# The last batch of a six-stage decoder kernel: the first half's feed forward placed beside the second attention's last part, and more side steps beside the part before it

## The chip, the cores and the metric

The kernel runs on one core of a Trainium2 chip. The metric is the device time of one execution in microseconds (us), as the median of several runs. One execution was also taken by the hardware profiler; its instructions, waits and transfers are what the views quoted below show. Engines are named as the profile names them: PE (TensorE, matmul), PEld (its weight loads), DVE (VectorE), ACT (ScalarE), POOL (GpSimd), SP (SyncE, here a queue of transfers).

## The reference

Input x has 4 batches of 1024 tokens with 256 channels. Two layers follow, each with a self attention, a cross attention to 77 context tokens and a feed forward, all with a layer norm before them and a residual add after. What the change touches is the second layer:

```python
x = x + _L1_attn_ref(_layernorm(x), L1_attn_W)            # 16 heads, |q.k|^2 times a decay, causal
x = x + _L1_xattn_ref(_layernorm(x), ctx_768, ...)        # 8 heads, softmax over 77 context tokens
x = x + _L1_ffn_ref(_layernorm(x), w_gate, w_up, w_down)  # 256 -> 704 -> 256

def fp4_linear(x, w):                                     # blocks of 16, both sides rounded to FP4
    return jnp.einsum('bsk,nk->bsn', fp4_quant_dequant(x), fp4_quant_dequant(w))
...
h = jax.nn.silu(fp4_linear(x, w_gate)) * fp4_linear(x, w_up)
return fp4_linear(h, w_down)
```

The attention mixes tokens causally; the cross attention and the feed forward work on each token by itself. So the second half of a batch's tokens needs the first half in the attention, and nowhere after it.

## The kernel before

A tile is 128 tokens by 256 channels; a batch has eight, held in two halves of four (`X[b, 0]` and `X[b, 1]`). The stages are Python generators that emit instructions and yield after each *step*. `schedule` (end of the file) combines them: `weave(a, na, b, nb)` advances a and b so that after any number of steps their shares done/na and done/nb are level, `zip2` advances all its generators once per round, `chain` runs one after another, `take(g, n)` gives the next n steps of g. The text order that comes out is the planner's priority order: `TileContext(..., schedule_with_timeline_sim=True)` orders each engine's queue at build time, by a timeline of its own, among instructions whose inputs and buffers are ready there. On the chip each queue runs in that order.

The stages of the second layer:

- `A1` is the self attention, written as units of one key tile by a chunk of two query tiles. Chunk c has 2c+2 units; four head groups make a pass. For the last batch, b = 3, the passes are split: chunks 0 and 1 of all four groups first (24 units, the *short part*, first half of the tokens), then chunks 2 and 3 (56 units, the *long part*, second half). Per unit there are score matmuls (L898, banks S), absolute values (DVE L904, ACT L902), a square (ACT L906), on the diagonal a decay (POOL L909), and value matmuls (L927). Line L947 (POOL) adds a finished chunk of a group into X; there are eight in each part.
- `XA(b, 1, (half,))` is the cross attention of one half: layer norm, a transposed pair of high and low parts, then per tile a *head* (scores, eight exponentials on ACT, a division) and a *tail* (transposes, 15 matmuls, the residual add on DVE, L637). It is 9 steps.
- `F1(b, groups, alt, keep)` is the feed forward. Per group of nt tiles: layer norm on POOL (L206 to L212, L226), rounding to FP4 (`fp4`: L1005 to L1009 and L1011 to L1014, DVE, POOL and ACT in turns), transposes (L235). Per tile: *up*, 24 matmuls of 352 columns with a tanh, a copy and two products (L1094, L1095, L1097, L1099), FP4 rounding of the 704 values, and *down*: six transposes (L1109, L1113), their high and low parts (L179, L180), 18 matmuls of 256 columns, and the residual add on DVE, L1118. The group's store to `out` (L171) is issued after its last tile. A whole batch is 52 steps, a group of four alone 27, a group of two alone 15.
- `XF(K, b)` is what follows A1 for a batch: `XA` of half 0 (9 steps), then `XA` of half 1 zipped with the first 20 steps of `F1` (21 rounds), then the other 32 steps of `F1`: 62 steps.

`alt` renames the buffers that a stage uses, so that two can be under way at once. Lane banks are T and W (PSUM banks 4, 5, 6) by default, TB and WB (banks 0 to 3, which A1 uses for S, U and D) where `alt` has `ps` 1. `XL` gives the cross attention buffers of its own; `FL` has four sets for the feed forward: `FL[0]` is None (its own buffers xn, xX, E, xph, xpl, wst, kh, q4s), `FL[1]` puts the same into `ot`, `QS`, `V`, `y0`, `y1`, `P`, `KS`, `VsJ` with banks T and W, `FL[2]` and `FL[3]` use `DL`, `QS` or `KS`, `V`, `WAh`, `WAl`, `qp`, `P`, `VsJ` with banks TB and WB. QS, KS, P, VsJ, DL, y0, y1 and ot are A1's.

The last batch before the change, in text order:

1. Beside the short part: three units, then 21 units woven with 20 steps of `XF(2)`.
2. Beside the long part: three units, then the other units of A1 (weight 55) woven with the other 42 steps of `XF(2)`, zipped with `XA(3, 1, (0,))`: 43 rounds with weight 62, so they end in the text at about unit 38 of 55.
3. After A1: `XA(3, 1, (1,))` on banks TB and WB, then lanes 2 and 3 (feed forward of tiles 4, 5 and of tiles 6, 7) zipped; woven one to one with lanes 0 and 1 (tiles 0, 1 and tiles 2, 3) zipped.

Of the kernel before, what the change touches and what calls it, by code (L numbers as in the profile page):

```python
# [1136 lines left out]
def zip2(*gens):  # L1137
    gens = list(gens)
    while gens:
        for g in list(gens):  # L1140
            try:
                next(g)
            except StopIteration:
                gens.remove(g)
        yield


def run_all(g):
    for _ in g:
        pass  # L1150


def chain(*gens):
    for g in gens:
        yield from g


def take(g, n):
    for _ in range(n):
        if next(g, g) is g:  # L1160
            return
        yield


def weave(a, na, b, nb):

    live = {0: (a, na), 1: (b, nb)}
    done = [0, 0]
    while live:
        k = min(live, key=lambda k: done[k] / live[k][1])  # L1170
        try:
            next(live[k][0])
            done[k] += 1
        except StopIteration:
            del live[k]
        yield


def spill(K, b):
    K.n += 1  # L1180
    K.xs[b] = K.dr.tile([T, C], F32, name=f"xs{b}")
    for g in range(2):
        K.store_x(b, K.xs[b], g)
    yield


def XF(K, b):

    yield from K.XA(b, 1, (0,), K.XL)
    f1 = K.F1(b, keep=K.w1)  # L1190
    yield from zip2(late(lambda: K.XA(b, 1, (1,), K.XL, K.mu)), take(f1, 20))
    yield from f1
# [6 lines left out]
def schedule(K, nb):  # L1199
    K.prep_a0()  # L1200
    preps = chain(K.prep_x(0), K.prep_p0(), K.prep_x(1), K.prep_f0())
    front = K.A0_front(0, K.kept)
    run_all(take(front, NF0))
    K.prep_ctx()
    run_all(weave(front, 44 - NF0, take(preps, NP0), NP0))
    more = {1: K.prep_x(2), 2: chain(K.prep_a1(), K.prep_f1_up()), 3: K.prep_f1_down()}
    a1 = K.A1([(b, (0, 1, 2, 3)) for b in range(nb - 1)] + [(nb - 1, (0, 1)), (nb - 1, (2, 3))])
    for b in range(nb):
        seg = K.A0(b, K.A0_front(b + 1) if b + 1 < nb else chain(K.A1_front(0), take(a1, 1)))
        if b == 0:  # L1210
            side, n = preps, NS0
        else:
            side, n = chain(K.XA(b - 1, 0), K.F0(b - 1), spill(K, b - 1), more[b]), NS1[b - 1]
        run_all(weave(seg, 196, side, n))
    K.phase = 1
    for b in range(nb):
        side = chain(K.XA(nb - 1, 0), K.F0(nb - 1), spill(K, nb - 1)) if b == 0 else XF(K, b - 1)
        if b + 1 < nb:
            main = chain(take(a1, 44), weave(take(a1, 22), 22, K.A1_front(b + 1), 19), take(a1, 14))
            run_all(take(main, K.LAG1 + 1))  # L1220
            run_all(weave(main, 96, side, 85 if b == 0 else 68))
        else:
            run_all(take(a1, K.LAG1 + 1))
            xf = XF(K, b - 1)
            run_all(weave(take(a1, 21), 21, take(xf, 20), 20))
            run_all(take(a1, K.LAG1 + 1))
            run_all(weave(a1, 55, zip2(xf, K.XA(b, 1, (0,), K.XL)), 62))
    b = nb - 1

    def lanes(ks):  # L1230
        return zip2(*(K.F1(b, ((2 * k, 2),), K.FL[k], K.w1) for k in ks))

    run_all(weave(chain(K.XA(b, 1, (1,), {**K.XL, "ps": 1}), lanes((2, 3))), 1, lanes((0, 1)), 1))


def parts(K, phases, nb):
# [41 lines left out]
@with_exitstack  # L1278
def decoder_kernel(ctx, tc, ins, consts, out, phases=None, nb=B):
    K = Kern(ctx, tc, ins, out, consts, nb=nb)  # L1280
    if phases is None or len(phases) == 6:
        schedule(K, nb)
    else:
        parts(K, phases, nb)
# [41 lines left out]
```

## Time and profile before

| what | value |
|---|---|
| time, median of 3 runs | 2407.63 us |
| lowest and highest run | 2401.26, 2417.06 us |
| the profiled execution's own time | 2403.86 us |
| its span, first to last instruction | 2402.1 us |
| mean granted PE clock over the span | 0.955 |
| busy share of PE, DVE, ACT, POOL | 90%, 70%, 68%, 50% |
| last L947 (chunk of A1 added) of the short part | 2112.02 us |
| last L947 of the long part, the end of A1 | 2267.33 us |

The span runs from the first to the last instruction; the own time is 1.8 us more, the median of the runs 3.8 us more than the own time. In a row of the timeline the first number is the start in us from the span's start, the second the duration, then engine, line, operation, tiles written and read, shapes; brackets hold the idle time before it and what ended that. In the table by windows each row is a stretch, with the busy time of each engine in it and, at the end, the mean granted PE clock, the share of the DMA engines and GB/s.

### The profile page before, as it was taken

What the parts mean: (1) busy time and instruction counts of PE and PEld (TensorE: products, weight loads), DVE (VectorE), ACT (ScalarE), POOL (GpSimd) and SP (SyncE); (2) the same over time, 40 slices, a digit from 0 to 9 for tenths busy, and PEclk for the clock granted to TensorE, in tenths of its full rate; (3) what the DMA queues carried; (4) which work ended last, traced back from release to release, by engine and by line L of the source; (5) the groups of instructions that cost most, each with busy time, mean ns of one, the idle gap of its engine ahead of it and who ended that gap; (6) DMA issues with size and microseconds to landing.
All of it is one profiled execution on the core that took longest, in us unless ns stands there. A gap on an engine that the chain in (4) does not pass through costs nothing.

```text
span 2402.1 us, 51405 instructions
## 1 busy us (share of the span) xinstructions
PE 2150.0 (90%) x19073; PEld 1520.1 (63%) x19110; DVE 1688.9 (70%) x3781; ACT 1638.8 (68%) x4173; POOL 1196.0 (50%) x1942
## 2 busy tenths in 40 slices
PE   6798999998999998899988988889988998899886
PEld 5454457755667655576656766567766767676676
DVE  4666657677666787776765667777866777777775
ACT  4365446676766676565778878987678877887542
POOL 7121303154331352412545458766866787775664
PEclk9899999999999999899989999999999999899997
DMA  8677331224751236222262224412341223542000
GB/s 256 190 206 212 117 90 44 63 57 115 230 143 49 62 105 194 73 73 49 73 188 50 71 71 138 140 38 56 99 116 38 56 80 115 104 99 71 10 10 18
DMA packets 182697, 238.45 MB, mean 99 GB/s; under 512 B 16198, under 2 KB 165846, under 8 KB 175958
## 3 DMA queue, kind: packets, MB, share of 16 engines
q1 hardware_dynamic: 182446, 235.15, 34.9%
q8 instruction: 151, 2.47, 0.4%
q14 instruction: 100, 0.82, 0.1%
HBM read 152.62 MB, written 82.21 MB: 98 GB/s over the span
## 4 chain that ended last, share of the span: by engine, by line
PE 60%; DVE 13%; DMA 8%; ACT 7%; POOL 7%; issue 3%; SPq 1%; POOLq 0%; another core or an unknown queue 0%; ACTq 0%; DVEq 0%
PE T L191 10%; PE W L191 8%; PE O L413 7%; PE Q L191 5%; PE O L927 5%; PE S L401 4%; PE M L352 4%; PE S L898 3%; DVE P L904 2%; DVE s_mt L357 2%; PE W L630 1%; DMA wst<-in_L_xattn_Wq 1%; DMA KS<-c_alk 1%; ACT P L906 1%; PE T L723 1%
## 5 line engine op out<-in xcount | busy, mean ns | idle before, releaser
L357 DVE TENSOR_REDUCE s_mt<-M 128x1 f32<-128x512 f32 (+3 forms) x608 | 386.2, 656 | 135.1 <-PE M L356 97.3
L404 ACT ACTIVATE P<-S 128x512 f32<-128x512 f32 (+1 forms) x640 | 342.0, 562 | 152.3 <-PE S L401 77.0
L906 ACT ACTIVATE P<-P,eps 128x1024 f32<-128x1024 f32 x320 | 343.9, 1080 | 55.5 <-DVE P L904 52.6
L904 DVE TENSOR_REDUCE P<-S 128x512 f32<-128x512 f32 (+1 forms) x480 | 284.8, 611 | 78.2 <-PE S L898 58.6
L352 PE MATMUL M<-KS,QS 108*128 108x512 bf16 (+3 forms) x768 | 225.7, 339 | 47.8 <-DVE s_mt L357 24.6
L898 PE MATMUL S<-QS,KS 96*128 96x256 bf16 (+1 forms) x1280 | 219.4, 270 | 36.6 <-DVE P L904 34.1
L191 PE MATMUL T<-R,xX 128*128 128x352 f32 (+1 forms) x1136 | 246.5, 331 | 4.0 <-ACT E L619 1.4
L401 PE MATMUL S<-QS,KS 110*128 110x256 bf16 (+1 forms) x1280 | 230.4, 267 | 14.7 <-ACT P L404 12.4
L413 PE MATMUL O<-P,V 128*32 128x256 f32 (+1 forms) x2560 | 239.4, 376 | 0.5 <-ACT ot L427 0.2
L622 POOL TENSOR_TENSOR E<-E,s_xsm 128x616 f32<-128x616 f32 x64 | 77.8, 1217 | 323.9 <-DVE s_xsm L620 270.8
L191 PEld LDWEIGHTS T<-R,xX 128*128 128x128 f32 x1136 | 182.9, 190 | 24.1 <-ACT E L619 5.4
L191 PE MATMUL W<-R,xph 128*128 128x256 f32 (+1 forms) x952 | 184.8, 292 | 6.5 <-DVE xpl L180 4.8
L909 POOL TENSOR_TENSOR P<-P,y 128x512 f32<-128x512 f32 x128 | 164.8, 1296 | 31.8 <-ACT y L871 17.0
L619 ACT ACTIVATE E<-T,s_xmx 128x77 f32<-128x77 f32 x512 | 159.3, 333 | 28.1 <-DVE s_xmx L616 26.0
L927 PE MATMUL O<-P,VsJ 128*32 128x128 f32 x3584 | 170.4, 286 | 4.8 <-ACT P L906 3.8
L898 PEld LDWEIGHTS <-KS 96*128 96x128 bf16 x1280 | 102.1, 99 | 110.6 <-issue 88.9
L401 PEld LDWEIGHTS <-KS 110*128 110x128 bf16 x1280 | 106.9, 99 | 102.5 <-issue 58.6
L191 PEld LDWEIGHTS W<-R,xph 128*128 128x128 f32 (+1 forms) x952 | 149.1, 192 | 17.7 <-DVE xpl L180 6.6
L352 PEld LDWEIGHTS <-QS 108*128 108x128 bf16 x768 | 68.1, 99 | 126.5 <-issue 99.2
L191 PE MATMUL W<-R,xpl 128*128 128x256 f32 (+2 forms) x476 | 139.5, 293 | 0.8 <-DVE xpl L180 0.8
L730 POOL TENSOR_TENSOR R<-wst 128x256 f32<-128x256 f32 x128 | 92.9, 736 | 86.0 <-DVE wst L729 80.9
L179 ACT ACTIVATE xph<-W 128x512 fp32r<-128x512 f32 (+2 forms) x180 | 79.1, 457 | 83.1 <-PE W L633 34.0
(351 smaller groups left out, 5662.6 us busy)
## 6 DMA issues: line engine op xcount, KB each, us to landing
QS<-dr SPq DMA_DIRECT2D x144, 192.0 KB
KS<-dr SPq DMA_DIRECT2D x72, 384.0 KB
dr<-qp SPq DMA_DIRECT2D x32, 768.0 KB
MD<-R SPq DMA_DIRECT2D x24, 616.0 KB
UD<-R SPq DMA_DIRECT2D x24, 512.0 KB
R<-MD SPq DMA_DIRECT2D x32, 308.0 KB
X<-in_x SPq DMA_DIRECT2D x16, 512.0 KB
dr<-qp SPq DMA_DIRECT2D x32, 256.0 KB
```

Source lines behind the costliest of these rows:

```text
L191: nc.tensor.matmul(out, x, y, start=first and n == 0, stop=last and n == len(seq) - 1)
L352: nc.tensor.matmul(Sv[:, x, 0:w], QS[:108, i // 4, hh, i % 4 * 128 : i % 4 * 128 + 128], KS[:108, hh, k0:k1], start=x == 0, stop=not diag ...
L357: nc.vector.tensor_reduce(out, Sv[:, :, 0:w], AX.X, ALU.max)
L401: nc.tensor.matmul(S[:, e, 0:w], st[1][:110, hh, j * 128 : (j + 1) * 128], st[0][:110, q0 // 512, hh, q0 % 512 : q0 % 512 + w], start=e == ...
L404: nc.scalar.activation(P[:, 2 * p : 2 * p + 2, 256 - w :], S[:, :, 0:w], AF.Exp)
L413: nc.tensor.matmul(O[0][hh * 32 : hh * 32 + 32, o + o0 : o + 256], V[j // 4][:, j % 4, h * 17 : h * 17 + 32], P[:, hh, o0:], start=c % 2 = ...
L619: nc.scalar.activation(E[:, n * 77 : (n + 1) * 77], Sv[:, k, :], AF.Exp, bias=mx[:, n : n + 1], accum_out=sm[:, n : n + 1])
L898: nc.tensor.matmul(S[:, e, 0:w], st[r][1][:96, hh, j * 128 : (j + 1) * 128], st[r][0][:96, q0 // 512, hh, q0 % 512 : q0 % 512 + w], start= ...
L904: nc.vector.tensor_reduce(Pv, S[:, :, 0:w].unsqueeze(3), AX.X, ALU.max, apply_absolute_value=True)
L906: nc.scalar.activation(Pw, Pw, AF.Square, bias=self.eps1)
L909: nc.gpsimd.tensor_tensor(Pd, Pd, Ds[r, c][:, j - 2 * c], ALU.mult)
L927: nc.tensor.matmul(Oc[rows, o0 : o0 + 128], lhs, P[:, hh, c0 : c0 + 128], start=j == 2 * c and i == 2 * c, stop=fin and i == 2 * c + 1)
```

## The change

Three edits, all in `schedule`, for the last batch alone:

```diff
             xf = XF(K, b - 1)
-            run_all(weave(take(a1, 21), 21, take(xf, 20), 20))
+            run_all(weave(take(a1, 21), 21, take(xf, 36), 36))
             run_all(take(a1, K.LAG1 + 1))
-            run_all(weave(a1, 55, zip2(xf, K.XA(b, 1, (0,), K.XL)), 62))
+            side = chain(zip2(xf, K.XA(b, 1, (0,), K.XL)), K.F1(b, ((0, 4),), keep=K.w1))
+            run_all(weave(a1, 55, side, 57))
     b = nb - 1
 
-    def lanes(ks):
-        return zip2(*(K.F1(b, ((2 * k, 2),), K.FL[k], K.w1) for k in ks))
-
-    run_all(weave(chain(K.XA(b, 1, (1,), {**K.XL, "ps": 1}), lanes((2, 3))), 1, lanes((0, 1)), 1))
+    f1 = [K.F1(b, ((2 * k, 2),), K.FL[k], K.w1) for k in (2, 3)]
+    run_all(chain(K.XA(b, 1, (1,), {**K.XL, "ps": 1}), zip2(*f1)))
```

Beside the short part 36 steps of `XF(2)` are woven in place of 20: all of both cross attention halves, the feed forward of batch 2's first half, and the start of that of its second. Beside the long part there are the other 26 steps zipped with `XA(3, 1, (0,))` (27 rounds), then the feed forward of batch 3's first half as one group of four tiles in the default buffers (27 steps): 54 rounds with weight 57, so they end in the text at about unit 52 of 55. After A1 there are only `XA(3, 1, (1,))` and then lanes 2 and 3. `FL[0]` and `FL[1]` are used no more. The arithmetic is the same. The first half has one layer norm over four tiles in place of two over two, and one store in place of two.

## Prediction

> **What bounds the kernel now.** First the page: which engine is full, and where it stops being full.
>
> ```profile
> span 2402.1 us, 51405 instructions
> PE 2150.0 (90%) x19073; PEld 1520.1 (63%) x19110; DVE 1688.9 (70%) x3781; ACT 1638.8 (68%) x4173; POOL 1196.0 (50%) x1942
> ...
> PE   6798999998999998899988988889988998899886
> ...
> PEclk9899999999999999899989999999999999899997
> ```
>
> PE is the bound (90% busy, nines and eights in the slices) until the last slices, which fall to 8 and 6. Only the last 350 us are touched. Second, the table by windows, cut at the ends of A1's parts (2112 and 2267.3):
>
> ```profile
> 2055.00:2074.00 19.00, 17.62 (x195) 14.34 (x195) 13.97 (x37) 16.98 (x42) 16.93 (x29) 1.00 0.42 90
> 2074.00:2093.00 19.00, 15.70 (x183) 9.60 (x181) 15.75 (x36) 16.66 (x38) 16.59 (x32) 0.73 0.65 138
> 2093.00:2112.00 19.00, 18.26 (x199) 14.38 (x199) 14.05 (x39) 17.55 (x49) 13.67 (x23) 1.00 0.55 111
> 2112.00:2196.00 84.00, 81.22 (x893) 65.37 (x891) 62.97 (x140) 69.72 (x178) 58.40 (x104) 0.98 0.37 88
> 2196.00:2267.30 71.30, 64.34 (x723) 47.27 (x722) 55.99 (x120) 50.73 (x76) 39.74 (x67) 0.98 0.08 28
> 2267.30:2278.00 10.70, 4.56 (x28) 3.83 (x26) 6.13 (x14) 2.36 (x5) 10.06 (x18) 0.81 0.00 1
> 2278.00:2340.00 62.00, 51.34 (x337) 48.85 (x338) 45.34 (x101) 28.89 (x108) 42.47 (x60) 0.89 0.03 10
> 2340.00:2369.00 29.00, 22.66 (x141) 20.96 (x140) 24.18 (x40) 13.41 (x28) 19.74 (x16) 0.94 0.03 10
> 2369.00:2402.10 33.10, 20.04 (x102) 18.27 (x102) 12.31 (x25) 5.11 (x11) 8.78 (x7) 0.66 0.07 24
> ```
>
> The first busy column is PE. In the long part it is 81.22 + 64.34 = 145.6 of 155.3 us (94%): whatever is put there lengthens it almost one for one. In the 134.8 us after A1, the *tail*, it is 98.6 us (73%): 36 us are empty. The short part has one soft place, 2074 to 2093, with PE at 15.7 of 19 us and the clock at 0.73.
>
> Third, the timeline, for who is late:
>
> ```profile
> 2148.33 0.42 DVE L1118 SCALAR_TENSOR_TENSOR X<-W,X 128x256 f32<-128x256 f32 x1 [1.57 <-PE W L191]
> ...
> 2259.01 0.41 DVE L1118 SCALAR_TENSOR_TENSOR X<-W,X 128x256 f32<-128x256 f32 x1
> ...
> 2267.33 0.46 POOL L947 TENSOR_TENSOR X<-X,yy 128x128 f32<-128x128 f32 x1 [3.25 <-DVE yy L945]
> ...
> 2293.68 0.42 DVE L1118 SCALAR_TENSOR_TENSOR X<-W,X 128x256 f32<-128x256 f32 x1 [0.80 <-PE W L191]
> ...
> 2332.57 0.42 DVE L637 TENSOR_TENSOR X<-X,WB 128x256 f32<-128x256 f32 x1 [0.75 <-PE WB L191]
> ...
> 2398.45 0.42 DVE L1118 SCALAR_TENSOR_TENSOR X<-WB,X 128x256 f32<-128x256 f32 x1 [4.30 <-PE WB L191]
> ```
>
> The feed forward of batch 2 adds its first tile at 2148.3, its fifth at 2259.0, and its eighth at 2293.7, 26 us after A1 (2267.3), although the text ends it at unit 38 of 55. So the lane lags behind its text, at (2259.0 - 2148.3)/4 = 27.7 us a tile beside A1 and (2293.7 - 2268.6)/2 = 12.5 us a tile after it. The tail is a chain: A1's last chunk, the second half's cross attention (last add 2332.6), lane 3 (last add 2398.5).
>
> **The change part by part.** I write A for the time of A1's last L947 and price what stands before and after it.
>
> *Removed from the tail: lanes 0 and 1.* From the PE groups in the tail, lane 1 (two tiles): up, 48 matmuls, 9.5 us; down, 24 + 12 matmuls, 3.2 + 1.8 us; transposes of h 1.3 + 0.8 us; of x 0.7 us. That is 17.3 us, 8.65 a tile, 34.6 us for four tiles. With them goes batch 2's rest: 12 ups of the 60 in that row (11.4 us), 2.3 us; 46 down matmuls at lane 1's 5.0 us per 36, 6.4 us; two tiles' transposes, 2.1 us: 10.8 us. In all 45.4 us of PE that the text now puts ahead of A.
>
> *Added beside A1.* If all of it ran before A, A would move by 45.4/0.937 = 48.5 us; what spills over (s us) stays in the tail. How much spills follows from the lane. It starts earlier: the first head of the second half's cross attention ran at 2072.9 to 2077.1, its next score matmul at 2097.6, and the first up at 2099.0, with 36 steps in place of 20 ahead of the same units. From the empty 3.3 us of 2074 to 2093 and half of its 10.2 us at clock 0.50, at most 8 us are to be had; I take 5, the lower end being nothing. ACT, at 51.2 of 57 us in the short part, is the reason not to take all. But then the lane needs eight tiles of batch 2 at 20 us (from 2208.6 to 2268.6 it did three, with no cross attention beside it) to 27.7 us, so by A only about one of the four new tiles can be done: s = 26 us, ends 0 (all done) and 45 (nothing moved). A = 2267.3 + (45.4 - 26)/0.937 - 5 = 2283.
>
> *The tail after A.* Three pieces. Layer norm, 2267.3 to 2281.9, 14.6 us, of which POOL spent 6.1 us on the lanes' products; with one lane about 12, ends 8 and 14.6. Cross attention, 2281.9 to 2332.6, 50.7 us: its first two adds came 18.5 and 23.1 us after the norm, the third 20.2 us after the second, with both lanes' ups between. Undisturbed, three more at the 4.6 us between the first two give 32; one lane in place of two stands beside it now, so I take 41, half way, ends 32 and 50.7. Lane 3 from 2332.6 to 2398.9, 66.3 us, of which 36 beside lanes 0 and 1, which end at 2368.6. Its floor is 43: 16.5 us until its first up is under way at 2349, two tiles' ups 9.5, a rounding 7.0 (one tile's L1005 to L1014 in a row), copy and product 1.4, transposes to the first down matmul 3.7 (2383.7 to 2387.4), the last down and its add 4.6. Lane 2 stays beside it, so I take 54, ends 43 and 66.3. Then 3.2 us to the span's end. Sum 12 + 41 + 54 + 3.2 = 110.2, ends 86 and 134.8.
>
> *Small edits.* One norm in place of two takes seven POOL operations away (L206 to L212, 1.7 us); it is hidden behind the lane's wait. One store of 512 KB in place of two: SP's last stores stand behind one another anyway. It now comes ahead of the cross attention's six MD and UD loads in the text; before, these were issued at 2182.7 to 2203.5, long ahead of batch 2's stores (2239.3 on) that also precede them in the text, so I cost this at nothing; queued behind the store they would come with the lane's end, at most the norm's 12 us late.
>
> *A new wait* is the shared xn: the norm of the second half's cross attention and the new group take the same single buffer. The new group gives it back after its transposes. If the lane is so late that this falls after A, the cross attention waits, at most the 17 us that norm, rounding and transposes took batch 2's first group (2077.9 to 2095 us); I take nothing, since the fifth tile of batch 2 was out before A already. The two-deep E and wst buffers carry one lane in both kernels.
>
> *Sum.* 2283 + 110 = 2393 for the span, 9 under 2402.1; own time 2403.86 - 9 = 2395. The runs' median stood 3.8 above the own time, so **2398 us**.
>
> A rule beside it: the Trainium skill, "TensorE: Matmul & The Clock Gate", section "Part 1: The HAM clock gate", has the PE clock at either half or full rate, full only after some 3.4 us of sustained work. This speaks against the change, since it empties the tail. The rows show the same kind of thing (0.50 from 2082.8 to 2093.0 and from 2383.2 to the end, where 18 down matmuls took 4.2 us against 2.1). By the rule taken to its end, lanes 2 and 3 at half rate throughout, an estimate from lane 1's price adds 17.3 us and gives 2415; by the row (0.66 in the last 33 us, 0.89 to 0.94 before) the tail already pays it.
>
> **The rivals.**
> 1. *Slower: all is absorbed ahead of A.* The planner gives the lane its place in the text, and s = 0. At 0.90 (64.34 of 71.3, one lane beside A1) A = 2267.3 + 45.4/0.90 = 2317.7; the tail, without fillers and at half clock, stays at 110. Span 2428, median 2433. For: A1 is later in the text than the lane. Against: the lane's lag above. It ends above before from the point where A moves by over 134.8 - 110.2 = 24.6 us.
> 2. *Faster: the tail drops to its floor.* 8 us from the soft place (A = 2280) and 86 us of tail: span 2366, median 2372. For: three streams share DVE and POOL from 2278 to 2369 (DVE 24.2 of 29 us), two will. Against: one of the three stays.
> 3. *It does not do what it says.* The lane lags so that all four tiles run after A, in one lane in place of two, beside the same cross attention. A 2267 to 2272 and the tail as before: median 2408 to 2412. For: batch 2's three late tiles. Against: the earlier start.
>
> **How the numbers follow.** Forecast 0.48; rival 1, 0.18; rival 2, 0.17; rival 3, 0.17. Within 1%, about what a measurement of this kernel can tell from no change, is 2383.6 to 2431.7. Faster by over that: rival 2 and a fifth of the forecast's own spread, 0.26. Slower: two thirds of rival 1 and a little of the others' upper ends (the xn wait, half clock), 0.16. The same: 0.58. The forecast's own range, s from 10 to 40 with its tail held, is 2384 to 2416; to hold 8 in 10 the range goes on to the edge of rival 2 and into rival 1: 2373 to 2431.
>
> **What would show it.** Right: the last L947 at 2275 to 2295; batch 2's eighth L1118 near or before it; one to two of batch 3's first four L1118 ahead of it, the others within 50 us; the last L637 some 53 us after A and the last L1118 some 107 after. In 2074 to 2093 the clock near 1.00. Wrong towards rival 1: A beyond 2300 and the tail's clock under 0.75. Towards rival 3: A as before and none of the four adds ahead of it. A tail of over 120 us with few fillers would mean that my price of the cross attention or lane 3 without neighbours is wrong, most likely the half clock or the shared xn.

## The result and the profile after

| | before | after |
|---|---|---|
| median of 20 runs each | 2407.41 us | 2414.65 us |
| lowest and highest | 2395.71, 2417.06 us | 2408.28, 2421.52 us |
| ratio to before, 95% interval | | 1.0036 [1.0023, 1.0049] |
| span of the profiled execution | 2402.1 us | 2413.4 us |
| end of batch 2's A1 to the end of the span | 349.7 us | 357.0 us |
| of it: short part, long part, tail | 59.7, 155.3, 134.7 us | 59.8, 165.0, 132.2 us |
| lane matmuls in the long part, in the tail | 299, 451 | 312, 438 |

The change costs 7.2 us between the medians, 8.7 by the ratio. The row that the rest of this text goes by is the *stretch*, from batch 2's last L947 to the end of the span: it began between 2050.8 and 2065.3 us in the profiled executions, which no edit here explains, so its length says more than its end. How well does the length repeat? Four pairs of kernels whose schedules came out almost alike (after and e9, e10 and e13, e14 and e15, e11 and e12 of the table below) have 357.0 and 356.2, 349.4 and 349.8, 351.7 and 352.3, 391.8 and 391.4 us. But in four others (before, e7, e8, e16) PE, DVE, ACT and POOL run the long part in the same order, instruction by instruction, and it took 155.3, 156.6, 154.3 and 152.7 us. Each is one execution, so a difference under some 4 us is not read as one here unless other runs repeat it. The stretch is 7.3 us longer. A *lane matmul* is an up (24 a tile), a down (18) or one of the six transposes of h: 48 a tile.

The page of the changed kernel, to be held against the page before:

```profile
span 2413.4 us, 51427 instructions
PE 2160.5 (90%) x19110; PEld 1523.1 (63%) x19110; DVE 1690.4 (70%) x3779; ACT 1638.9 (68%) x4171; POOL 1192.8 (49%) x1935
...
PE   6798999998999998899988988889988998998886
...
PEclk9899899999999998899999999999989999999988
```

Nothing stands out here: the same shares, the same soft end. The page doesn't show the change; the stages do. The table by windows of the changed kernel, cut at the short part, the long part and the tail (first busy column PE, near the end the granted PE clock):

```profile
2056.50:2116.20 59.70, 54.51 (x599) 40.53 (x598) 46.26 (x117) 52.64 (x128) 51.06 (x87) 0.91 0.52 111
2116.20:2281.20 165.00, 150.54 (x1627) 114.87 (x1626) 123.47 (x269) 121.44 (x256) 103.66 (x183) 0.97 0.22 56
2281.20:2413.40 132.20, 96.39 (x592) 89.10 (x590) 84.62 (x168) 48.43 (x147) 69.50 (x79) 0.85 0.04 13
```

PE is busy 150.54 of 165.0 us in the long part (91%; before 145.6 of 155.3, 94%): 5.0 us more work, 4.7 us more idle time. The tail still has 96 us of PE. The same cut, for the matmuls that read the feed forward's weights alone (tile R; the transposes are not in it, so 42 a tile). The kernel before:

```profile
2052.37:2112.02 59.65, 3.77 (x18) 2.94 (x18) 0.00 (x0) 0.00 (x0) 0.00 (x0) 0.91 0.52 109
2112.02:2267.33 155.31, 45.59 (x263) 37.93 (x264) 0.00 (x0) 0.00 (x0) 0.00 (x0) 0.98 0.24 60
2267.33:2402.10 134.77, 68.40 (x393) 62.68 (x392) 0.00 (x0) 0.00 (x0) 0.00 (x0) 0.84 0.04 13
```

The changed kernel, long part and tail:

```profile
2116.20:2281.20 165.00, 49.07 (x276) 41.36 (x277) 0.00 (x0) 0.00 (x0) 0.00 (x0) 0.97 0.22 56
2281.20:2413.40 132.20, 66.70 (x380) 61.14 (x378) 0.00 (x0) 0.00 (x0) 0.00 (x0) 0.85 0.04 13
```

Of the 391 matmuls that start in the old tail (the row's 393 has two that were under way at its edge) the text moves 223 ahead of A1's end: four tiles of batch 3 (168) and batch 2's last 55. 13 went (263 to 276). The short part has 18 before, and 18 after. So the move that the diff writes hardly took place, and the timeline of the changed kernel says the same:

```profile
2152.04 0.42 DVE L1118 SCALAR_TENSOR_TENSOR X<-W,X 128x256 f32<-128x256 f32 x1 [0.93 <-PE W L191]
...
2300.01 0.42 DVE L1118 SCALAR_TENSOR_TENSOR X<-W,X 128x256 f32<-128x256 f32 x1 [1.56 <-PE W L191]
...
2326.47 0.42 DVE L1118 SCALAR_TENSOR_TENSOR X<-W,X 128x256 f32<-128x256 f32 x1
...
2346.15 0.41 DVE L637 TENSOR_TENSOR X<-X,WB 128x256 f32<-128x256 f32 x1
...
2364.76 0.42 DVE L1118 SCALAR_TENSOR_TENSOR X<-W,X 128x256 f32<-128x256 f32 x1 [2.70 <-PE W L191]
...
2409.73 0.42 DVE L1118 SCALAR_TENSOR_TENSOR X<-WB,X 128x256 f32<-128x256 f32 x1 [2.48 <-PE WB L191]
```

A, the last L947, is at 2281.19. Batch 2's first tile is added at 2152.04, 35.8 us after the short part's end (before: 36.3), its eighth at A+18.8, all four tiles of batch 3's first half after it (A+45 to A+84), the second half's cross attention ends at A+65, the last lane at A+128.5.

### The profile page after: what moved, and what is told of

It reads as the page before. It is cut to its first block, busy times and chain, and to the rows that moved or that the text cites. A ratio compares the mean times of both kernels' runs of the same rounds, so it can differ in the third digit from the quotient of the medians.

```text
span 2413.4 us, 51427 instructions
## 1 busy us (share of the span) xinstructions
PE 2160.5 (90%) x19110; PEld 1523.1 (63%) x19110; DVE 1690.4 (70%) x3779; ACT 1638.9 (68%) x4171; POOL 1192.8 (49%) x1935
## 4 chain that ended last, share of the span: by engine, by line
PE 61%; DVE 14%; DMA 7%; ACT 7%; POOL 6%; issue 3%; SPq 1%; POOLq 0%; DVEq 0%; ACTq 0%
PE T L191 10%; PE W L191 9%; PE O L413 7%; PE Q L191 5%; PE O L927 5%; PE S L401 5%; PE M L352 4%; PE S L898 3%; DVE P L904 2%; DVE s_mt L357 2%; DMA wst<-in_L_xattn_Wq 1%; PE T L723 1%; PE W L630 1%; ACT P L906 1%; PE M L356 1%
## 5 line engine op out<-in xcount | busy, mean ns | idle before, releaser
L404 ACT ACTIVATE P<-S 128x512 f32<-128x512 f32 (+1 forms) x640 | 342.2, 563 | 150.4 <-PE S L401 78.6
L191 PE MATMUL T<-R,xX 128*128 128x352 f32 (+1 forms) x1184 | 255.8, 332 | 5.8 <-DVE xpl L180 1.8
L191 PEld LDWEIGHTS T<-R,xX 128*128 128x128 f32 x1184 | 190.3, 190 | 27.2 <-issue 5.8
L191 PE MATMUL W<-R,xph 128*128 128x256 f32 (+2 forms) x976 | 194.5, 297 | 6.5 <-DVE xpl L180 4.7
L909 POOL TENSOR_TENSOR P<-P,y 128x512 f32<-128x512 f32 x128 | 164.8, 1295 | 34.0 <-ACT P L906 18.3
L191 PEld LDWEIGHTS W<-R,xph 128*128 128x128 f32 (+2 forms) x976 | 157.7, 197 | 18.2 <-DVE xpl L180 7.2
L191 PE MATMUL W<-R,xpl 128*128 128x256 f32 (+2 forms) x488 | 145.3, 298 | 1.0 <-DVE xpl L180 0.8
```

The costliest lines, as they stand in the source:

```text
L191: nc.tensor.matmul(out, x, y, start=first and n == 0, stop=last and n == len(seq) - 1)
L404: nc.scalar.activation(P[:, 2 * p : 2 * p + 2, 256 - w :], S[:, :, 0:w], AF.Exp)
L909: nc.gpsimd.tensor_tensor(Pd, Pd, Ds[r, c][:, j - 2 * c], ALU.mult)
```

## Experiments

There are eighteen further kernels, and the table has every one; "long" counts lane matmuls of 48 a tile, and each ratio stands with its 95% interval against the kernel before.

| kernel | ratio | stretch | long part, tail (us) | long |
|---|---|---|---|---|
| before | 1 | 349.7 | 155.3, 134.7 | 299 |
| after | 1.0036 [1.0023, 1.0049] | 357.0 | 165.0, 132.2 | 312 |
| e1 short edit alone | 1.0030 [1.0012, 1.0049] | 356.3 | 164.5, 132.1 | 311 |
| e2 move alone | 1.0022 [1.0006, 1.0037] | 352.3 | 160.4, 132.0 | 324 |
| e3 both norms in V | 1.0029 [1.0013, 1.0045] | 356.5 | 166.5, 130.5 | 287 |
| e4 other order, 33 steps | 1.0049 [1.0030, 1.0069] | 364.2 | 169.3, 134.8 | 313 |
| e5 first half left out | 0.9903 [0.9874, 0.9933] | 320.2 | 157.2, 103.1 | 312 |
| e6 bank of its own | 1.0096 [1.0066, 1.0126] | 372.4 | 162.0, 150.4 | 325 |
| e7 second half ahead | 1.0031 [1.0007, 1.0054] | 355.1 | 156.6, 138.6 | 299 |
| e8 first half ahead | 1.0043 [1.0022, 1.0064] | 358.9 | 154.3, 144.8 | 299 |
| e9 side early in the text | 1.0033 [1.0019, 1.0047] | 356.2 | 164.4, 132.1 | 312 |
| e10 new group, own buffers | 1.0006 [0.9988, 1.0023] | 349.4 | 164.4, 125.4 | 312 |
| e11 second group, own buffers | 1.0182 [1.0157, 1.0207] | 391.8 | 212.6, 119.4 | 430 |
| e12 e11 and e9 | 1.0191 [1.0167, 1.0215] | 391.4 | 212.8, 119.0 | 430 |
| e13 second norm in V | 1.0001 [0.9983, 1.0018] | 349.8 | 164.8, 125.4 | 312 |
| e14 rounding hoisted | 1.0008 [0.9989, 1.0026] | 351.7 | 172.7, 119.4 | 348 |
| e15 e14 and e13 | 1.0004 [0.9983, 1.0026] | 352.3 | 173.4, 119.3 | 348 |
| e16 before, second norm in V | 1.0016 [0.9994, 1.0039] | 355.3 | 152.7, 142.5 | 299 |
| e17 move alone, second norm in V | 0.9984 [0.9966, 1.0002] | 350.8 | 160.6, 130.5 | 324 |
| e18 e14 with 20 steps | 1.0004 [0.9986, 1.0022] | 354.0 | 170.5, 123.8 | 342 |

### The two halves of the change, each alone

e1 has only the first edit (36 steps for 20, beside the old four lanes); e2 only the other two.

```diff
# e1: before, with
-            run_all(weave(take(a1, 21), 21, take(xf, 20), 20))
+            run_all(weave(take(a1, 21), 21, take(xf, 36), 36))
# e2: after, with 20 steps again, and
-            run_all(weave(a1, 55, side, 57))
+            run_all(weave(a1, 55, side, 74))
```

> Only the first edit: 36 steps beside the short part, the rest as before (four lanes after the attention). Theory N (the shared norm buffer xn): with 36 steps the norm of batch 2's second feed-forward group comes ahead of the norm of batch 3's first cross attention in the text, takes the single xn and keeps it until its transposes, so that cross attention's norm starts some 80 us after the short part's end in place of 9 us, its last add about 55 us later, and the kernel is 0.2 to 0.5% slower than before (ratio 1.002 to 1.005). Rival L (one lane in place of two): the loss of the change comes from four tiles running in one lane after the attention, so this edit alone loses nothing: ratio 0.997 to 1.000.

> Only the second and third edit: 20 steps beside the short part as before, batch 3's first half in one lane behind the others beside the long part (weight 74 for its 70 rounds), two lanes after the attention. N: the first cross attention's norm comes some 10 us after the short part again; only the second wait is left, the norm of the second half's cross attention some 20 us after the attention's end in place of 15: ratio 0.999 to 1.002. L: the whole loss is here: ratio 1.003 to 1.006, with a tail of about 132 us.

e1 alone loses 6.6 us of stretch, with the old four lanes still there. e2 stands 2.6 us longer, which the stretch alone would not show, but its ratio is clear of 1; it lies between its two forecasts. So the steps moved up beside the short part are a loss by themselves, and they bring nothing into the short part: 59.6 us and 18 of the lane's weight matmuls, as before. The long part grows by 9.2 us for 12 more lane matmuls. What the trace shows of why: the first half's cross attention, which had its norm 9.6 us after the short part's end and its last add at A-66, has them at 84.8 us and A-18 in e1 (84.8 and A-19 in the change), and batch 2's second group now stands ahead of it in the text. Before, it stood beside the long part's first 90 us; in the change it comes late, and the lane still runs dry between its groups. The kernel before:

```profile
2112.00:2198.40 86.40, 83.62 (x915) 67.11 (x914) 64.24 (x143) 71.56 (x180) 59.04 (x106) 0.98 0.36 86
2198.40:2224.90 26.50, 23.11 (x290) 14.88 (x287) 22.02 (x45) 19.92 (x27) 17.11 (x32) 0.94 0.16 51
2224.90:2267.30 42.40, 38.83 (x414) 30.65 (x414) 32.70 (x74) 28.97 (x46) 22.00 (x33) 1.00 0.04 14
```

The changed kernel:

```profile
2116.20:2173.10 56.90, 53.19 (x577) 41.62 (x576) 43.48 (x96) 41.88 (x88) 36.20 (x72) 1.00 0.31 76
2173.10:2202.00 28.90, 23.15 (x289) 14.58 (x287) 22.22 (x48) 22.28 (x32) 21.35 (x36) 0.88 0.29 58
2202.00:2281.20 79.20, 74.20 (x765) 58.68 (x765) 57.77 (x126) 57.28 (x138) 46.11 (x77) 0.98 0.14 40
```

The middle row of each is the hole from one group's last up to the next group's first: norm, FP4 rounding and transposes of four tiles, with little but A1 on PE (80% in the changed kernel, clock 0.88). The kernel before has this hole too (26.5 us, 87%). PE's idle time in the three rows is 2.8, 3.4 and 3.6 us before and 3.7, 5.8 and 5.0 us after, so it grew in all three, and most in the hole. That the late cross attention is the cause of e1's loss is read from the trace and not shown; the next runs, which tried to bring the cross attention forward again, did not settle it.

### Bringing the first half's cross attention forward

```diff
# e3: after, both second-layer cross attentions of batch 3 with "xn": "V" (not the shared xn)
# e4: after, 33 steps, and the cross attention first in each round
+            side = chain(zip2(K.XA(b, 1, (0,), K.XL), xf), K.F1(b, ((0, 4),), keep=K.w1))
# e6: after, its norm in V and its transposes and products on bank 6 alone, the lane on banks 4 and 5
```

> The change, with the norms of both of batch 3's cross attentions written to a buffer of tag V in place of xn. N: the first of them starts 10 to 30 us after the short part's end and the second 8 to 15 us after the attention's end; ratio to before 0.994 to 0.999, at least 0.5% under the change. L: nothing changes, ratio 1.003 to 1.005.

> The change with 33 steps in place of 36 and with the cross attention named first in the zip, so that its norm stands ahead of the second group's norm in the text; no buffer is added. N: the first wait is gone and the second stays: ratio 0.998 to 1.001. L: ratio 1.003 to 1.005 as with the change.

> The change, with the first cross attention of batch 3 on bank 6 alone (the feed forward keeps 4 and 5 in this part) and its norm in a buffer of tag V. Theory B (the banks are handed out in text order, so a cross attention that stands in the text beside the fifth feed-forward tile cannot overtake it, whatever its norm's buffer): its last add comes 40 us or more earlier relative to the short part's end than with the buffer alone (there 151 us), at 90 to 110 us. Rival N (only the norm's buffer holds it): it stays at 140 to 155 us. The time may go either way, since the lane has a bank fewer: ratio 0.996 to 1.006.

Theory N gave the right numbers for e1 (the norm 84.8 us after the short part's end, ratio 1.0030), but its reason, that the shared xn holds the first half's cross attention, fell here. In e3 its norm starts 37 us after the short part's end, not 84.8, in e4 after 7.8; but its transposes still wait. Its last add, 146 us after the short part's end in the change, comes at 151 us in e3, later and not earlier, and at 134 us in e4. No time is gained; e4, with the earliest adds of the three, has the longest stretch, and its hole between the groups is 39.5 us. In the change and in e3 these transposes run right behind those of batch 2's second group (change: 2191.95 and 2200.20, then 2205.04; e3: 2200.74 and 2207.60, then 2212.34), and with a bank of their own in e6 they do so again (2204.72, then 2208.15). There the last add came at 179 us, later than both forecasts, and the tail, with one bank less for the lane, is 18 us longer. Whether bank 6 was still held in e6 by work that stands earlier in the text, the trace doesn't show. What holds that cross attention stays open.

### What the tail costs without the work that was to leave it

```diff
# e5: before, with the first half stored as it stands, without its feed forward
+    K.store_x(b, K.out[b], 0)
+    run_all(chain(K.XA(b, 1, (1,), {**K.XL, "ps": 1}), lanes((2, 3))))
# e7: before, the last weave 2 to 1 for the second half; e8: 1 to 2
```

> The kernel before with the feed forward of batch 3's first half left out (its four tiles are stored as the cross attention leaves them), so that after the attention only the second half's cross attention and two lanes run. It measures the tail's floor. Theory C (the tail is a chain of the attention's last chunk, the cross attention and two lanes that hardly notices the work beside it): the tail stays at 115 to 130 us where it was 134.7, ratio 0.992 to 0.998. Rival P (the prediction's price: neighbours stretch the chain, its floor is 86 to 110 us): the tail falls to 86 to 110 us, ratio 0.980 to 0.990.

> The kernel before with the last weave at 2 to 1 for the second half's cross attention and its two lanes, in place of 1 to 1. C: the chain is the limit and gets its place earlier, the cross attention's last add comes at 45 to 58 us after the attention's end in place of 65, and the end 5 to 12 us earlier: ratio 0.995 to 0.998. P: the sum of the work counts and the order does little: ratio 0.999 to 1.001.

> The same weave at 1 to 2: the first half's lanes go ahead. C: the chain starts later, 5 to 12 us slower, ratio 1.002 to 1.005. P: ratio 0.999 to 1.001.

The tail of e5, all engines, and then its lane matmuls:

```profile
2277.90:2381.00 103.10, 68.02 (x392) 61.81 (x390) 55.25 (x112) 34.83 (x116) 50.49 (x60) 0.81 0.03 11
...
2277.90:2381.00 103.10, 40.11 (x212) 37.69 (x210) 0.00 (x0) 0.00 (x0) 0.00 (x0) 0.81 0.03 11
```

With lanes 0 and 1 gone the tail is 103.1 us, 31.6 less than before, for the 34.6 us of PE that the prediction gave their four tiles; the stretch is 29.5 us shorter, the time 23 us by the ratio (16 to 30 by its interval). The price of a tail emptied of these four tiles (110, ends 86 and 134.8) was sound. Batch 2's last tiles still end in this tail (A+21), so a move that takes them out as well could spare more. The clock in this emptied tail is 0.81, against 0.84 before. The order within the tail isn't bettered by these two weights: 1 to 1 beats 2 to 1 by 3.9 us of tail and 1 to 2 by 10.1, and the ratios of both are clear of 1. For 1 to 2 theory C's forecast held. For 2 to 1 neither did: the second half's cross attention ended earlier (A+53.6 in place of A+65.2), as C has it, but the tail ended later. So this chain alone doesn't set the tail.

### Why the lane is late

```diff
# e9: after, with
+            run_all(weave(a1, 55, side, 110))
# e10: after, the new group with buffers of its own
+            side = chain(zip2(xf, K.XA(b, 1, (0,), K.XL)), K.F1(b, ((0, 4),), {"xn": "V", "xX": "QS"}, K.w1))
# e11: after, in F1: batch 2's second group with alt = {"xn": "V", "xX": "QS"}
# e12: e11 with weight 110
```

> The change with the weight of the side at 110 in place of 57: in the text all 54 side rounds are out by about unit 27 of 55, not 52. Theory T (place in the text): the lane is late because its instructions stand behind A1's in the order of priority. Then at least 60 of the lane's matmuls more than the change's 312 run in the long part, A's end moves by 10 us or more to 175 us and beyond after the short part's end, and the tail falls from 132 to under 122 us. Theory G (the lane runs dry at the bounds of its groups): the lane's own chain of norm, rounding, transposes and one shared buffer for the transposed group limits it, not its place: 312 to 330 matmuls, long part 163 to 168 us, tail 130 to 133 us, the time within 0.3% of the change's.

> The change with batch 3's first half normed into V and transposed into QS in place of the lane's xn and xX, so that its norm, rounding and transposes need not wait for batch 2's second group to have read its last transposed tile. Theory G (gaps at the bounds of groups): the last of the lane's gaps goes; the new group's first up follows batch 2's last up within 5 us (in the change 29 us or more), its first four adds come 15 to 25 us earlier relative to A (in the change A+45, 57, 72, 84), and up to 24 more of its matmuls run before A. The time: with the second half's cross attention as the chain of the tail 0 to 8 us less than the change. Theory T (place in the text): the new group stands last in the text, so its adds stay within 8 us of those of the change, and so does the time.

> The change with batch 2's second group of four tiles normed into V and transposed into QS; the new group then finds the lane's xn and xX free as well, so neither bound of groups in the long part has a shared buffer. Theory G (gaps): the hole of 28.9 us between the first group's last up and the second group's first is under 12 us; the lane is 17 to 25 us ahead, 40 to 90 more of its matmuls run in the long part (352 to 400 against 312), A moves 5 to 15 us later, the tail falls to 112 to 122 us. Whether that pays: by the prediction's own prices (8.65 us of PE a tile at a share of 0.93 to 0.94 ahead of A, 36 us empty behind it) the time falls 3 to 10 us below the change. Theory T: no hole goes, since the norms and transposes are late by their place: 312 to 330 matmuls and the time of the change.

> The second group's own buffers and the weight of 110 at once. If G and T both hold, the most of the planned 192 matmuls (four tiles of 48) runs ahead of A: 400 to 500 lane matmuls in the long part, the long part 175 to 195 us, the tail 103 to 112 us, as without the first half's feed forward (103). By the prediction's prices the span is then 5 to 12 us under that of the kernel before. If moving pays nothing because PE is full beside A1, the long part grows by as much as the tail falls and the time stays within 0.3% of the change's. If only T holds it equals the run with the weight alone, if only G holds the run with the buffers alone.

e9 refutes the place in the text: with the side's text out by unit 27, not 52, the same 312 matmuls run in the long part, the order on the engines there is the same, and so is the stretch to 0.8 us. So it isn't the order of priority that holds the lane; the planner has nothing of it ready to put ahead. e11 and e12 got the matmuls ahead (430) but were spoilt by their own edit. QS has two buffers, and A1 takes one for each of its four head groups. Issues of A1's QS loads in e11 (the timeline of SP's queue):

```profile
2163.18 1.85 SPq L323 DMA_DIRECT2D QS<-dr  x4
...
2232.43 1.77 SPq L323 DMA_DIRECT2D QS<-dr  x4
...
2274.41 1.77 SPq L323 DMA_DIRECT2D QS<-dr  x4
```

In the change the three are at 2108.1, 2152.3 and 2190.5. A1 waits for the lane, and from 2160 to 2190 PE has 14.47 of 30 us. So the time of e11 and e12 says nothing about the lane. e10 gave the whole loss back, but not as expected: the lane's adds came later (A+59 to A+95, not 15 to 25 us earlier), the hole between batch 2's last up and the new group's first grew from 18.5 to 28.6 us, and the tail shrank because the second half's cross attention came 18 us earlier. That pointed at its norm.

### The shared xn in the tail, and the rounding

```diff
# e13: after, with
-    run_all(chain(K.XA(b, 1, (1,), {**K.XL, "ps": 1}), zip2(*f1)))
+    run_all(chain(K.XA(b, 1, (1,), {**K.XL, "ps": 1, "xn": "V"}), zip2(*f1)))
# e14: after, the lane's three groups in one generator, and in F1
             for i in range(nt):
+                if i == nt - 1 and m + 1 < len(groups) and len(groups) > 2:
+                    nxt = prep(*groups[m + 1])      # layer norm and fp4 of the next group
# e15: e14 with e13's edit. e16: before with e13's edit.
```

> The change with the second half's cross attention alone normed into V, not into the shared xn. Theory X (the shared xn delays the tail's chain): its norm is applied 8 to 10 us after A1's end in place of 19.4, its last add comes at A+50 to A+55 in place of A+65, the last lanes end 5 to 8 us earlier relative to A, and the ratio to the kernel before is 0.999 to 1.002. Theory Y (the new group's lane fills what the cross attention leaves, and the tail ends no earlier): the norm comes as early, but the lanes still end at A+125 to A+130 and the ratio stays at 1.002 to 1.004.

> The change with the lane's three groups in one generator, and the layer norm and FP4 rounding of the next group put ahead of the last tile of the group before it. No buffer is added. Theory G (the lane runs dry at the bounds because norm and rounding start only there): the hole between the first group's last up and the second's first falls from 28.9 to under 15 us, the one at the new group likewise; the lane's adds of batch 3's first half come 15 to 35 us earlier relative to A (A+45, 57, 72, 84 in the change), 20 to 70 more of its matmuls run in the long part, A 3 to 12 us later, the tail 8 to 20 us shorter. The time by the prediction's prices: 0 to 8 us under the change. Theory R (the lane is limited within a tile: two E and wst buffers, rounding of the 704 values): the holes go, but the tiles come no faster, fewer than 20 more matmuls, the time within 0.2% of the change's.

> The hoisted rounding and the second half's norm in V together. If both G and X hold, the sum of the two: the second half's cross attention ends at A+45 to A+55, batch 3's first half at A+50 to A+65, the tail 110 to 120 us, the long part 168 to 178 us, and the ratio to the kernel before 0.993 to 1.000. If neither holds: the time of the change.

> The kernel before with the second half's cross attention normed into V. There the norm was applied 11.2 us after A1's end, ahead of lane 0's norm at 19.2. Theory X: the xn wait costs the kernel before little, since batch 2's last transposes were long done; the norm comes at 6 to 11 us, the lanes end within 4 us, ratio 0.998 to 1.001. Theory Y: the same. Should the tail fall by more than 5 us (ratio under 0.998), the chain of the cross attention sets the end in the kernel before as well, and this is the better version of it.

Theory X holds for the change. Its POOL rows after A (2281.19), from the timeline: the new group has taken xn, the second half's statistics are ready, and the norm is applied 14 us later.

```profile
2268.15 2.81 POOL L226 TENSOR_SCALAR xn<-X,s_lnw,s_lnrs 128x256 f32<-128x256 f32 x4
...
2286.39 0.20 POOL L212 TENSOR_SCALAR s_lnw<-s_lnmv 128x4 f32<-128x4 f32 x1
...
2298.59 1.06 POOL L1014 TENSOR_TENSOR xn<-xn,q4s 128x512 f32<-128x512 f32 x1 [2.26 <-DVE xn L1013]
2300.60 2.18 POOL L226 TENSOR_SCALAR xn<-X,s_lnw,s_lnrs 128x256 f32<-128x256 f32 x4 [0.95 <-PE T L235]
```

The bracket of the last row says for whom it waited: PE's transposes (L235) of the new group, the last reader of xn. The bracket holds only 0.95 us, because POOL did other work meanwhile; the wait is seen by taking the rows of one tile together. In e13, A at 2283.68:

```profile
2288.90 0.20 POOL L212 TENSOR_SCALAR s_lnw<-s_lnmv 128x4 f32<-128x4 f32 x1
2289.20 2.17 POOL L226 TENSOR_SCALAR V<-X,s_lnw,s_lnrs 128x256 f32<-128x256 f32 x4
...
2301.24 1.08 POOL L1014 TENSOR_TENSOR xn<-xn,q4s 128x512 f32<-128x512 f32 x1 [1.95 <-DVE q4s L1006]
```

And what follows in e13:

```profile
2331.08 0.40 DVE L637 TENSOR_TENSOR X<-X,WB 128x256 f32<-128x256 f32 x1
...
2405.40 0.43 DVE L1118 SCALAR_TENSOR_TENSOR X<-WB,X 128x256 f32<-128x256 f32 x1 [2.48 <-PE WB L191]
```

The norm follows its statistics at once (A+5.5, not A+19.4), the cross attention ends at A+47.4 (A+65.0), the last lane at A+121.7 (A+128.5). The stretch falls from 357.0 to 349.8, the ratio from 1.0036 to 1.0001, in intervals that don't overlap. e10, which frees xn from the other side, has the same stages to 0.4 us, so its QS added nothing. The cross attention's 17.6 us are not all gained: the lanes behind it, which had 63.6 us in the change, take 74.3, and the first half's adds come later (A+59 to A+95, not A+45 to A+84).

How much the wait is worth depends on what stands around it. e3 removes it as well and is 0.5 us shorter than the change; what differs there is that 25 fewer lane matmuls ran ahead of A (287), which the tail has to do. That this is the reason isn't shown.

e14 shows what a larger move is worth. The lane weights alone, long part and tail of e13 and then of e14:

```profile
2118.80:2283.70 164.90, 49.13 (x276) 41.54 (x277) 0.00 (x0) 0.00 (x0) 0.00 (x0) 0.97 0.22 56
2283.70:2409.10 125.40, 64.15 (x380) 58.76 (x378) 0.00 (x0) 0.00 (x0) 0.00 (x0) 0.86 0.04 13
...
2113.30:2285.90 172.60, 54.91 (x305) 45.38 (x306) 0.00 (x0) 0.00 (x0) 0.00 (x0) 0.98 0.21 54
2285.90:2405.40 119.50, 60.41 (x350) 55.98 (x349) 0.00 (x0) 0.00 (x0) 0.00 (x0) 0.83 0.04 14
```

The first hole falls from 28.9 to 12.2 us and the second, at the new group, from 28.7 in e13 to 16.7; 36 more of the lane's matmuls run ahead of A, and xn is free in time (norm at A+5.2). So theory G was right that the bounds of groups make the lane late. But beside e13, where xn is out of the way too, the long part grows by 7.9 us and the tail shrinks by 6.0: the two differ by less than single executions tell apart, so the exchange is even at best as far as these runs show. e15 adds nothing, as e14 had freed xn already.

e16: in the kernel before the norm stays at A+11.2, so the shared xn cost it nothing there. The tail is 7.8 us longer, with the lanes in another order; which part of that does it isn't shown, and the ratio's interval reaches below 1. The ratio of 1.0016 misses the forecast, and this is no better version.

### The candidates

e17 is e2 with the second norm in V; e18 is e14 with 20 steps beside the short part and weight 74.

> The move alone (20 steps beside the short part, weight 74 beside the long part) with the second half's cross attention normed into V. The move alone stood at 1.0022, its first-half lane after A1. If the shared xn is worth its 7 us here as well: ratio 0.998 to 1.000, the tail 124 to 128 us, the long part about 160. If moved work only costs ahead of A1's end what it spares behind it, the ratio stays within 0.999 to 1.002: no form of the move gains more than the interval.

> The hoisted rounding with 20 steps beside the short part and weight 74. With 36 steps: long part 172.7, tail 119.4, ratio 1.0008. If the 36 steps cost 4 us of their own (the first half's cross attention 25 to 45 us later): ratio 0.997 to 0.999 and the long part some 4 us shorter at the same tail. If the exchange is one for one whatever the order: 0.9995 to 1.002.

e17 has the lowest ratio, 0.9984 [0.9966, 1.0002]; its interval holds 1, and its stretch is 1.1 us longer than before. Its tail, 130.5 us, misses the forecast of 124 to 128. Against e2, which it differs from by the one norm, the second half's cross attention ends at A+51.8 in place of A+65.4; the stretch is 1.5 us shorter, while the ratio falls from 1.0022 to 0.9984 in intervals that don't overlap. The two measures disagree here, and how much the norm is worth in e2 stays open. e18 is even (1.0004), with a stretch 4.3 us longer. No version is shown to beat the kernel before. The 36 steps don't add up with the other edits either: they cost 6.6 us alone and 4.7 on the move (e2 to after), but nothing that these lengths show with the second norm in V (e17 to e13, -1.0) or with the hoist (e18 to e14, -2.3).

## Why the prediction was wrong, by its steps

The sum said 9 us less of span; the change costs 8.7 us by the ratio of the times and 7.3 by the stretch, so the direction is wrong, though the time itself, 2414.65, lies in the range. The gap between the two, some 16 us, is the tail's 22.0 us over its price, less the 5.9 us by which A moved too little (9.8 us, counted from the stretch's start, in place of 15.7). Of the 22.0 us, 6.8 go with the wait for xn (e13). The other 15.2 are put down to work that stayed in the tail and was not charged there, by e13's tail against e5's.

- **Bound: right.** It is PE, and what goes beside A1 lengthens it: by 7.9 us for 36 matmuls in e14.
- **"I take 5" from the soft place: nothing came.** In the changed kernel, shifted by the 4.1 us by which its stretch began later:

```profile
2078.10:2097.10 19.00, 15.54 (x184) 9.40 (x181) 16.03 (x36) 16.66 (x38) 16.57 (x32) 0.75 0.71 144
```

 The row before had 15.70 and 0.73. The added steps did not start sooner: the lane's first add comes 35.8 us after the short part's end, 36.3 before. What stands there is the norm, rounding and transposes of batch 2's first group (2077.9 to 2095 us before).
- **"s = 26, ends 0 and 45": it was 43.** 13 of 223 matmuls moved, and 45.4 x 210/223 = 42.8 us stayed. The lane's lag was seen, but its own rates were not carried through. From a first add 36 us after the short part's end, seven more at 20 to 27.7 us each end 176 to 230 us after it, and the prediction gave the long part 171; a start 5 us sooner would bring the eighth just to A. So by these rates none of the four new tiles could be done by A. The measured spacing is 21.1 us ((2300.0 - 2152.0)/7; before 20.8), the hole of 28.9 us at the bound of groups included.
- **A = 2283: right in size, not in reason.** 2281.2, or 2277.1 less the 4.1 by which the stretch began later; that it is so near is in part luck. 19.4 us of moved work were to make it; 13 matmuls moved. Of the 9.7 us by which the long part grew the lane's weight matmuls are 3.5 (49.07 - 45.59), other PE work is 1.5, and 4.7 are idle PE.
- **The tail, 110.2: the step that failed.** It took 132.2. By its pieces, with what was taken: to the end of the norm 21.6 (12), cross attention 43.8 (41), lanes 63.6 (54), end 3.2 (3.2). In the first 9.6 us is the new wait that the prediction named: *"the cross attention waits, at most the 17 us ... I take nothing, since the fifth tile of batch 2 was out before A already"*. Batch 2 was the wrong thing to look at: the new group takes xn at A-13 and gives it back at A+19. The norm was ready to be applied 14.0 us before it was, and taking the wait away is worth 6.8 us of tail and 7.2 of stretch (e13, and e10 the same). The larger piece is in the sum's logic: 26 of the 45 us were let spill into the tail, while the tail was priced as if one lane beside it cost little. Without the first half's feed forward it is 103.1 (e5), with all of it and without the wait 125.4 (e13): 22 us that the price of 110 hardly had.
- **The sign.** Even without the xn wait no run shows a gain. By the prediction's own prices four tiles cost 34.6/0.937 = 36.9 us ahead of A (an estimate), and e5 shows that leaving them out spares 31.6 behind it. e13 to e14 is the same exchange on a smaller scale, 7.9 paid and 6.0 spared, and by itself not clear of an even one. The gain of 9 in the sum came only from spilled work that was charged in neither place, and from the 5 us of the soft place.
- **The clock rule.** The Trainium skill, "TensorE: Matmul & The Clock Gate", "Part 1: The HAM clock gate", has the clock fall when PE is not kept busy. The rows show lower clocks where PE has gaps (0.64 from 2346.2 to 2365.2 with PE busy 14.3 of 19 us, 0.88 in the 28.9 us hole), but the tail as a whole went from 0.84 to 0.85, since it was not emptied, and where it was emptied (e5) the clock is 0.81. That the estimate of 2415 by the rule meets the measured time is luck; its reason is not what happened.
- **Rivals.** Rival 3 came nearest: all four tiles after A in one lane, the tail about as before (132.2 to 134.7). It missed the long part's 9.7 us, and with it the last 2 to 3 us of the time. Rival 1 was wrong that all would run ahead of A (13 matmuls did); that such work costs more there than it spares behind is the way e14 (7.9 paid, 6.0 spared beside e13) and e18 (9.9 and 6.7 beside e17) lean. Rival 2 had no part.

What stays open: what holds the first half's cross attention back in e3 and e4, and how much of e1's 6.6 us is that. The costs of the edits don't add up either: e1 loses 6.6 us with no new group and its second norm applied at A+8.1, while e13, with the same 36 steps, loses nothing.

## What to carry to other kernels

Before a move out of a stage with idle time is priced, measure both ends of the exchange: leave the work out once (here 31.6 us of the tail spared), and set that against its time at the busy share where it is to go (36.9 by the estimate). Work that "spills" must be charged where it lands. And when a stage is moved next to another, list the single buffers that both take, and ask not whether the old user is done but when the *new* one gives each back: with one of them (xn) taken away, by one word in a dictionary, the measured loss of this change was gone (7.2 of 7.3 us of stretch), though with both norms moved (e3) it was not.

## What was not expected of the chip

- The last stretch began within a spread of 14.5 us (2050.8 to 2065.3) from execution to execution, though no edit touches what comes before it. Its length repeated within 0.8 us in four pairs of kernels, but the long part, run in the same order by four kernels, took 152.7 to 156.6 us. One profiled execution of each kernel does not tell 2 us apart.
- A PE with gaps also ran slower. In e11's hole, from 2160 to 2190, the clock was 0.67 at 14.47 of 30 us busy, and six up matmuls took 2.13 us; just ahead of it, from 2149.6 to 2154.3, six took 1.21 to 1.24.
